# Relative-position terms of an attention block: from tables in DRAM to slices of one table on chip

## The chip, the cores and the metric

The kernel runs on one core of one Trainium2 chip. The metric is the device time of one execution, in microseconds, as the median of several runs. The core has a tensor engine (PE; its weight loads are listed apart as PEld), a vector engine (DVE), a scalar engine (ACT), GpSimd (POOL), and queues that issue DMAs; SP issues nearly all of them here, ACT's queue a few.

## The reference, cut to what matters

The whole computation has four layers on an image of 48 x 48 tokens with 768 channels: an attention block with an MLP, a spectral layer (AFNO), a state-space scan, and a second spectral layer. Only the attention block's position terms are touched. With 12 heads of 64 channels:

```python
coords = jnp.arange(H)[:, None] - jnp.arange(H)[None, :] + (H - 1)
Rh = rel_pos_h[coords]            # (48, 48, 64), from a table of 95 rows
Rw = rel_pos_w[coords]
rel_h = jnp.einsum('bhwc,hkc->bhwk', r_q, Rh)
rel_w = jnp.einsum('bhwc,wkc->bhwk', r_q, Rw)
attn = (attn.reshape(B * nh, H, W, H, W) + rel_h[:, :, :, :, None] + rel_w[:, :, :, None, :])
```

So each query gives, for each head, 48 numbers by key row and 48 by key column. All queries in one image row use the same 48 rows of the first table, a window that slides by one from row to row; the same holds for image columns and the second table.

## The kernel before, in words

**The phases.** `qkv_phase` makes q, k, v and the position terms and writes them to DRAM; attention (`attention_bounded`) reads them back in chunks; projection, MLP and the other layers follow. Everything is float32 except the position terms, which are split into three bfloat16 parts.

**The qkv phase.** Tokens are in six blocks of 384, taken two at a time as three superblocks `sb`. For each superblock `v_rows` makes v (L164, in a seven-product scheme, 21 groups of three products each), and `q_and_k` makes q and k (L295) for six pairs of heads `pr`, seven groups of three products each. The products of these two lines have weights of 128 x 128 and 384 columns.

**The position terms.** When the q of a superblock begins to be made, `position_terms` puts 24 steps on a list: first 12 `rel_h` (three pairs of pairs `cp`, two blocks `n`, two halves `hh`), then 12 `rel_w` (four image columns each). A step needs four tables of 128 x 96, one for each of four positions: two copies of the 64 x 48 window on the diagonal, one per head of the pair, zeros elsewhere. The host lays them out in DRAM (`relD`), and `tables` (L379) loads four at a time. The step makes four products (L401 for `rel_w`, L415 for `rel_h`) with 96 columns of q each into one PSUM tile of tag `m` (six buffers, shared with q, k and v). `split` then makes the three bfloat16 parts: ACT copies (L371), DVE subtracts (L372), ACT copies again (L373), DVE subtracts again (L374), into the tile `rw` or `rh`, of each of which there is one buffer. After the last step of a group, `store` (L390) writes the tile to `rw_d` or `rh_d`.

`rel_h` takes columns of q with a step of 8 floats in memory; `rel_w` takes runs of 8 floats.

**The order.** One step at a time goes between groups of q/k or v products: `advance` runs the next step, and keeps three steps' tables loading ahead. In `q_and_k` it is called twice per pair from the third pair on, eight times in all; in `v_rows` of the next superblock, `between` calls it after each group until the list is empty. Of the last superblock eight steps run among its q/k products and 16 are left. The program is written in a layer that adds the waits and allots the buffers. [...]

**The end of the phase.** After the last q/k product, DVE reduces maxima of q, k and the tables (L462 to L471); one product (L475, `bound`) sums them; DVE makes a `flag` from it (L478), by which attention chooses its form. Then four steps are issued, the phase's left-side pools are closed, five steps follow, `ahead(1)` opens attention's buffers and loads its first chunk (one piece of q, eight loads of position terms: L519, L498, L499), and the last seven steps come. An earlier `ahead(0)` has loaded the first pair's keys and values (L514, L515). Attention's first products are L559; it then adds the position terms by a product with a one-hot matrix (L567), and multiplies the values (L588).

Of the kernel before, what the change touches and what calls it, by code (L numbers as in the profile page):

```python
# [20 lines left out]
P = 128  # L21
G = 48
T = G * G
C = 768
NC = C // P
NT = T // P
NH, HD = 12, 64
FF = 4 * C
NF = FF // P
TB = 384  # L30
# [147 lines left out]
            emit(*blocks[n], o)  # L178


def qkv_phase(tc, ident, x, qkv_w, qkv_b, relT, rel_d, ln_g, ln_b, q_d, k_d, v_d, rw_d, rh_d, wqk_d, wv_d, flag, home, ahead):

# [13 lines left out]
    nc = tc.nc  # L196
    V = nc.vector
    NSB = NTB // 2
    TS = 2 * TB
    with (  # L200
# [139 lines left out]
        with tc.tile_pool(name="qkv_v0", bufs=1, side="right") as vp:  # L340
            w = vp.tile([P, 7, NC2, TB], F32, tag="wv", name="wv")
            a21 = vp.tile([P, NC2, TB], F32, tag="a21", name="a21")
            load_x(0, 0)
            for k in range(2):
                nc.sync.dma_start(w[:, k], wv[:, k * NC2 : (k + 1) * NC2, 2 * C : 2 * C + TB])
            prepare(0, 0)
            load_x(0, 1)
            nc.sync.dma_start(w[:, 6], wv[:, NC2:, 2 * C + TB :])
            nc.sync.dma_start(a21, wv[:, :NC2, 2 * C + TB :])
            vb = load_bcast(nc, kp, qkv_b[2 * C : 3 * C], C, "vb")  # L350
            qkb = load_cols(nc, kp, qkv_b[0 : 2 * C], 2 * NC, "qkb")
            kb = kp.tile([P, NC], F32, tag="kb", name="kb")
            rel = qp.tile([P, 2, 2 * G - 1], F32, tag="rel", name="rel")
            for s in range(2):
                nc.sync.dma_start(rel[s * HD : (s + 1) * HD], relT)
            qms, kms = (qp.tile([P, NC, NSB], F32, tag=n, name=n) for n in ("qms", "kms"))
            prepare(0, 1)
            combine(nc.gpsimd, (w[:, 0], w[:, 1], a21, w[:, 6]), w[:, 3], w[:, 2], w[:, 5], w[:, 4])
            sums(0)
            V.tensor_scalar(kb, qkb[:, NC : 2 * NC], HD**-0.5, None, ALU.mult)  # L360
            v_rows(0, lambda n: w[:, n])
            nc.sync.dma_start(wv_d, w)

        with tc.tile_pool(name="qkv_o", bufs=1, side="right") as op:
            R = 2 * G

            def split(ps, parts, n):

                r = op.tile([P, TB], F32, tag="rest", name=f"rest_{n}", bufs=2)
                r = r[:R].rearrange("p (a b c) -> p a b c", a=ps.shape[1], b=ps.shape[2])  # L370
                nc.scalar.copy(parts[0], ps)  # L371
                V.tensor_tensor(r, ps, parts[0], ALU.subtract)  # L372
                nc.scalar.copy(parts[1], r)  # L373
                V.tensor_tensor(parts[2], r, parts[1], ALU.subtract)  # L374

            def tables(which, g, n):

                d = qp.tile([P, 4, R], F32, tag="relD", name=f"relD_{which}_{g}_{n}", bufs=4)
                nc.sync.dma_start(d, rel_d[which, g])  # L379
                return d  # L380

            def position_terms(sb, q):


                q6 = q.rearrange("p c b (j w h) -> p c b j w h", j=KJ, w=KTW)
                tiles = {}

                def store(d, at, cols):
                    for s in range(2):
                        nc.sync.dma_start(d[s, :, :, sb, cols], at[s * G : (s + 1) * G].rearrange("k n c b t -> k n (c b t)"))  # L390

                def rel_w(g):

                    if g == 0:
                        tiles["rw"] = op.tile([P, 3, NC, 2, TB], BF16, tag="rw", name=f"rw_{sb}")
                    d, at = tiles.pop(("w", g)), tiles["rw"]
                    ps = pm.tile([P, 512], F32, tag="m", name=f"rw_{sb}_{g}")
                    pv = ps[:R, :TB].rearrange("p (c b w h) -> p c b w h", c=NC, b=2, w=4)
                    j, w0 = divmod(4 * g, KTW)
                    for i in range(4):  # L400
                        nc.tensor.matmul(pv[:, :, :, i, :], lhsT=d[:, i, :], rhs=q6[:, :, :, j, w0 + i, :], start=True, stop=True)  # L401
                    cols = slice(j * P + w0 * KTH, j * P + (w0 + 4) * KTH)
                    split(ps[:R, :TB].rearrange("p (c b t) -> p c b t", c=NC, b=2), [at[:R, n, :, :, cols] for n in range(3)], f"w{sb}_{g}")
                    if g == G // 4 - 1:
                        store(rw_d, at, slice(0, NC * TS))

                def rel_h(cp, n, hh):

                    if (n, hh) == (0, 0):
                        tiles["rh"] = op.tile([P, 3, 2, 2, TB], BF16, tag="rh", name=f"rh_{sb}_{cp}")  # L410
                    d, at = tiles.pop(("h", cp, n, hh)), tiles["rh"]
                    ps = pm.tile([P, 512], F32, tag="m", name=f"rh_{sb}_{cp}_{n}_{hh}")
                    for i in range(4):
                        rhs = q6[:, 2 * cp : 2 * cp + 2, n, :, :, 4 * hh + i].rearrange("p c j w -> p c (j w)")
                        nc.tensor.matmul(ps[:R, i * 2 * G : (i + 1) * 2 * G], lhsT=d[:, i, :], rhs=rhs, start=True, stop=True)  # L415
                    rows = at[:, :, :, n, :].rearrange("p s c (w h) -> p s c w h", h=KTH)
                    split(ps[:R, :TB].rearrange("p (h c w) -> p c w h", h=4, c=2), [rows[:R, k, :, :, 4 * hh : 4 * hh + 4] for k in range(3)], f"h{sb}_{cp}_{n}_{hh}")
                    if (n, hh) == (1, 1):
                        store(rh_d, at, slice(2 * cp * TS, (2 * cp + 2) * TS))

                def load(key, *args):
                    tiles[key] = tables(*args, "_".join(str(k) for k in (sb, *key)))

                for cp in range(NC // 2):
                    for n in range(2):
                        for hh in range(2):
                            key = "h", cp, n, hh
                            steps.append((lambda key=key: load(key, 0, 2 * (2 * sb + key[2]) + key[3]), lambda key=key: rel_h(*key[1:])))
                for g in range(G // 4):
                    steps.append((lambda g=g: load(("w", g), 1, g), lambda g=g: rel_w(g)))  # L430

            steps, ready = [], []

            def advance():
                while len(ready) < 3 and steps:
                    load, run = steps.pop(0)
                    load()
                    ready.append(run)
                if ready:
                    ready.pop(0)()  # L440

            slots = [0]

            def between():

                left = len(steps) + len(ready)
                slots[0] = slots[0] or 20
                for _ in range(-(-left // slots[0])):
                    advance()
                slots[0] = max(slots[0] - 1, 1)  # L450

            for sb in range(NSB):
# [4 lines left out]
                if sb + 1 < NSB:  # L457
                    load_x(sb + 1, 0)
                q_and_k(sb, lambda q: position_terms(sb, q), advance)

            qm, km = (qp.tile([P, NC], F32, tag=n, name=n) for n in ("qm", "km"))
            V.tensor_reduce(qm, qms, axis=AX.X, op=ALU.max)  # L462
            V.tensor_reduce(km, kms, axis=AX.X, op=ALU.max)
            rm = qp.tile([P, 2], F32, tag="rm", name="rm")
            V.tensor_reduce(rm, rel, axis=AX.X, op=ALU.max, apply_absolute_value=True)
            V.tensor_scalar(km, km, rm[:, 0:1], rm[:, 1:2], ALU.add, ALU.add)
            pz = qp.tile([P, 2, NC], F32, tag="pz", name="pz")
            V.memset(pz, 0.0)
# [7 lines left out]
            mx = qp.tile([1, 1], F32, tag="mx", name="mx")  # L476
            V.tensor_reduce(mx, ps[:1, : 2 * NC], axis=AX.X, op=ALU.max)
            V.tensor_scalar(flag, mx, SAFE, None, ALU.is_lt)  # L478
            for _ in range(4):
                advance()  # L480
            inner.close()
            for _ in range(5):
                advance()
            ahead(1)
            while steps or ready:
                advance()


# [794 lines left out]
def block_kernel(ctx: ExitStack, tc: tile.TileContext, a: dict):  # L1283
    nc = tc.nc
# [35 lines left out]
        nc.vector.memset(ones, 1.0)  # L1320
        ahead.extend((loads, kvs, qbs, ones, oneh))

    qkv_phase(tc, ident, x, a["qkv_w"], a["qkv_b"], a["relT"], a["relD"], a["ln1_g"], a["ln1_b"], q_d, k_d, v_d, rw_d, rh_d, wqk_d, wv_d, flag, home, load_ahead)

    def opened(name, shape, side):
        stack = ExitStack()
# [446 lines left out]
def laid_out(i):  # L1773
# [5 lines left out]
        d[k] = i[l0 + k]  # L1779

    d["relT"] = np.stack([i[l0 + "rel_pos_h"][::-1].T, i[l0 + "rel_pos_w"][::-1].T], 1)

    rel = np.zeros((2, G, 2, HD, 2 * G), np.float32)
    for pos in range(G):
        for s in range(2):
            rel[:, pos, s, :, s * G : (s + 1) * G] = d["relT"].transpose(1, 0, 2)[:, :, G - 1 - pos : 2 * G - 1 - pos]
    d["relD"] = rel.reshape(2, G // 4, 4, P, 2 * G).transpose(0, 1, 3, 2, 4)
# [34 lines left out]
```

## Time and profile before

| What | Value |
|---|---|
| Median of 3 runs | 3837.66 us (3835.54 to 3838.72) |
| The profiled execution's own time | 3841.45 us |
| Its span in the profile | 3839.7 us |
| Mean granted clock of PE | 0.986 of full |
| PE busy | 3727.7 us, 97% of the span |
| DVE / ACT / POOL busy | 2057.3 / 1142.8 / 656.5 us |
| Bytes moved by DMA | 460.43 MB, mean 120 GB/s |
| qkv phase | about 0 to 512 us |
| of it, the part after the last q/k product | 478.7 to 511.6 us |

A line of a group names the source line, engine, operation, tile written and tiles read, shapes (partitions x elements; for a product the weights' rows * columns first), and the number of instructions; behind the bar stand its busy time in us, the mean ns of one, and the engine's idle time before it with what ended that. A float32 product leaves two records. Records of PE overlap[...]; the distance from start to start is what a product costs in a full stream. A line of the order in time has start, length, engine, source line and count, and in brackets the idle time before it. A chain of waits is read back from the last instruction, at each step to what released it.

### The profile page before, as it was taken

The page shows a single profiled execution, that of the slowest core. Times are in us where ns is not written, and L with a number is a line of the kernel's source. Part 1 is how long each engine was busy: PE and PEld are TensorE (multiplying, and loading weights), DVE is VectorE, ACT ScalarE, POOL GpSimd, SP SyncE. Part 2 cuts the span into 40 slices and gives each one's busy share as a digit, 9 for nine tenths or more (in the row PEclk, how much of TensorE's full clock was granted, in tenths as well). Part 3 has the DMA queues.
Part 4 walks back from the last instruction along what each step waited for, and adds up shares of the span by engine and source line. Part 5 has one row for each costly group of instructions (what it writes and reads, how often), then busy time and mean ns, then how long its engine had stood idle before and what let it go on. Part 6 is the DMA issues. An engine that isn't in the chain of part 4 may idle for free.

```text
span 3839.7 us, 54414 instructions
## 1 busy us (share of the span) xinstructions
PE 3727.7 (97%) x22018; PEld 2255.4 (59%) x22018; DVE 2057.3 (54%) x3184; ACT 1142.8 (30%) x1908; POOL 656.5 (17%) x498
## 2 busy tenths in 40 slices
PE   7999979999999999999999999999999998999998
PEld 4666544444444444445555555555568876996685
DVE  6655456666666666555524332323325567995455
ACT  1323234444444444420310120012013356222341
POOL 3101001111111111015000000000013311981131
PEclk9999989999999999999999999999999999999999
DMA  7656563333232322124434534443454312112345
GB/s 254 211 193 194 178 184 119 113 107 128 84 112 75 115 74 91 42 71 139 151 104 136 173 107 121 133 137 104 125 166 105 108 36 93 40 33 73 97 114 155
DMA packets 266762, 460.43 MB, mean 120 GB/s; under 512 B 32941, under 2 KB 219301, under 8 KB 260007
## 3 DMA queue, kind: packets, MB, share of 16 engines
q1 hardware_dynamic: 256695, 435.93, 37.0%
q10 hardware_dynamic: 9808, 20.94, 1.5%
q8 instruction: 175, 2.87, 0.3%
q14 instruction: 84, 0.69, 0.1%
HBM read 318.49 MB, written 138.31 MB: 119 GB/s over the span
## 4 chain that ended last, share of the span: by engine, by line
PE 93%; DVE 2%; DMA 2%; issue 1%; ACT 1%; POOL 1%; SPq 0%; DVEq 0%; ACTq 0%; POOLq 0%
PE p L867 13%; PE p L930 12%; PE s L559 12%; PE av L588 12%; PE c L1183 6%; PE s L567 6%; PE qk L295 6%; PE c L1094 4%; PE v L164 3%; PE pj L164 2%; PE f_z L1489 2%; PE f_z L1488 2%; PE f_x L1453 2%; PE so L1263 2%; PE f_u L1503 2%; PE rh L415 1%
## 5 line engine op out<-in xcount | busy, mean ns | idle before, releaser
L577 DVE TENSOR_TENSOR acc<-acc,p 128x768 f32<-128x768 f32 x576 | 584.1, 1014 | 355.1 <-ACT p L569 317.1
L569 ACT ACTIVATE p<-s 128x768 f32<-128x768 f32 x648 | 478.6, 812 | 693.7 <-PE s L567 581.2
L930 PE MATMUL p<-w,h 128*128 128x384 f32 x1512 | 492.7, 486 | 0.0
L559 PE MATMUL s<-qt,kv 64*128 64x384 f32 x2592 | 478.5, 501 | 9.9 <-ACT p L569 7.7
L588 PE MATMUL av<-p,kv 128*64 128x384 f32 x2592 | 464.5, 493 | 0.0
L930 PEld LDWEIGHTS p<-w,h 128*128 128x128 f32 x1512 | 286.1, 190 | 196.9
L559 PEld LDWEIGHTS s<-qt,kv 64*128 64x128 f32 x2592 | 233.1, 187 | 250.6 <-ACT p L569 116.3
L588 PEld LDWEIGHTS av<-p,kv 128*64 128x64 f32 x2592 | 170.0, 136 | 225.2 <-issue 215.2
L867 PE MATMUL p<-x2nT,w 128*128 128x384 f32 x864 | 294.2, 490 | 3.4 <-issue 3.4
L295 PE MATMUL qk<-xnT,wqk 128*128 128x384 f32 x756 | 251.8, 490 | 5.3 <-DMA wqk<-wqk_d 5.3
L1183 PE MATMUL c<-H,bands 128*48 128x96 f32 x5632 | 242.2, 247 | 12.4 <-issue 12.4
L567 PE MATMUL s<-bt,oneh 120*128 120x384 bf16 x1296 | 249.1, 329 | 0.0
L1183 PEld LDWEIGHTS c<-H,bands 128*48 128x48 f32 x5632 | 234.6, 123 | 20.2 <-issue 12.7
L867 PEld LDWEIGHTS p<-x2nT,w 128*128 128x128 f32 x864 | 165.5, 192 | 119.5 <-issue 6.3
L867 PE MATMUL p<-xT,w 128*128 128x384 f32 x648 | 220.7, 486 | 0.0
L567 PEld LDWEIGHTS <-oneh 120*128 120x128 bf16 x1296 | 109.3, 98 | 174.6 <-issue 116.1
L295 PEld LDWEIGHTS qk<-xnT,wqk 128*128 128x128 f32 x756 | 144.3, 192 | 99.6 <-issue 7.9
L906 POOL TENSOR_TENSOR rr<-rr,ml_b 128x1152 f32<-128x1152 f32 x12 | 31.9, 2661 | 957.6 <-DMA rr<-xr_d 677.5
L862 ACT ACTIVATE h<-h,ml_b 128x384 f32<-128x384 f32 x144 | 88.3, 615 | 346.8 <-DVE h L882 174.3
L1191 POOL TENSOR_TENSOR t<-s,c 128x768 f32<-128x768 f32 x80 | 144.6, 1831 | 178.7 <-DVE s L1154 167.6
L867 PEld LDWEIGHTS p<-xT,w 128*128 128x128 f32 x648 | 123.1, 190 | 85.9
L597 DVE RECIPROCAL rec<-rs 128x384 f32<-128x384 f32 x36 | 92.1, 2558 | 100.6 <-PE rs L595 100.6
(323 smaller groups left out, 4800.6 us busy)
## 6 DMA issues: line engine op xcount, KB each, us to landing
w<-w1s_d SPq DMA_DIRECT2D x36, 768.0 KB
w<-w2s_d SPq DMA_DIRECT2D x36, 768.0 KB
bt<-rh_d SPq DMA_DIRECT2D x144, 162.0 KB
w<-w1s_d SPq DMA_DIRECT2D x36, 576.0 KB
w<-in_mlp_w_dram SPq DMA_DIRECT2D x27, 768.0 KB
wqk<-wqk_d SPq DMA_DIRECT2D x12, 1344.0 KB
yu<-f_ys SPq DMA_DIRECT2D x24, 672.0 KB
f_gt<-yu SPq DMA_DIRECT2D x24, 672.0 KB
```

The source lines that it names most:

```text
L164: nc.tensor.matmul(p[:, :TB], lhsT=rhs[n][:, c, t * P : (t + 1) * P], rhs=w[:, c, :], start=c == 0, stop=c == NC2 - 1)
L295: nc.tensor.matmul(p[:, :TB], lhsT=w[:, n, c, :], rhs=ops[sb][n][:, c, :], start=c == 0, stop=c == NC2 - 1)
L559: nc.tensor.matmul(ps[:, s, :QB], lhsT=keys[pr % 2][rows, kt * P : (kt + 1) * P], rhs=qbs[qc % 2][0][rows], start=True, stop=False)
L567: nc.tensor.matmul(ps[:, s, :QB], lhsT=oneh[:NBR, b % 3, :], rhs=qbs[qc % 2][1][:NBR, s, b // 3, j, :], start=False, stop=True)
L569: nc.scalar.activation(p, ps[:, :, :QB], AF.Exp)
L577: nc.vector.tensor_tensor(probs[c], probs[c], p, ALU.add)
L588: nc.tensor.matmul(avs[c][rows, :QB], lhsT=vals[pr % 2][:, kt, rows], rhs=p[:, s, :], start=kt == 0, stop=kt == NT - 1)
L867: nc.tensor.matmul(p[:, :TB], lhsT=w[n][:, c, :], rhs=rhs[n][:, c, :], start=c == 0, stop=c == NC2 - 1)
L930: nc.tensor.matmul(ps[t][:, :TB], lhsT=hs[left, f][:, t * P : (t + 1) * P], rhs=wt[:, f % KW2, :], start=f == 0, stop=f == NF2 - 1)
L1094: nc.tensor.matmul(ps[:K, i, :n], lhsT=v[:, c, tok : tok + K], rhs=w[:, cc, c0 : c0 + n], start=cc == NC - 1, stop=cc == 0)
L1183: nc.tensor.matmul(ps[r0 : r0 + G, k // 4, cols], lhsT=bands[:, n - GC, i, :] if gr else bands0[:, n, i, :], rhs=H[:, n, :, d : d + NPR], ...
L1191: GP.tensor_tensor(t, sc[:, ch], c1[:, m0 : m0 + GC].unsqueeze(2).to_broadcast([P, GC, RR, NPR]), ALU.mult)
```

## The change

The tables in DRAM go. Both tables of 95 entries (`relT`) stand on chip already, once on each half of the partitions, for the bound. They are now padded with 16 columns of zeros to 111, and a window of 64 columns is taken from them as weights, starting at the position in question; 48 of its 64 results are used. Where one product with a 128 x 96 table stood, two stand with weights of 64 x 64, one for each head of the pair: partitions 0 to 63 into PSUM partitions 0 to 63, and 64 to 127 into 64 to 127, of the same PSUM tile. The splits take all 128 partitions, and the stores take partitions 0 to 47 and 64 to 111.

At the end of the phase six steps now stand ahead of the bound's reductions and product; the pools are closed and `ahead(1)` follows at once, and ten steps come after it.

```diff
-            rel = qp.tile([P, 2, 2 * G - 1], F32, tag="rel", name="rel")
+            rel = qp.tile([P, 2, G - 1 + HD], F32, tag="rel", name="rel")
+            V.memset(rel[:, :, 2 * G - 1 :], 0.0)
             for s in range(2):
-                nc.sync.dma_start(rel[s * HD : (s + 1) * HD], relT)
+                nc.sync.dma_start(rel[s * HD : (s + 1) * HD, :, : 2 * G - 1], relT)
...
-                r = r[:R].rearrange("p (a b c) -> p a b c", a=ps.shape[1], b=ps.shape[2])
+                r = r.rearrange("p (a b c) -> p a b c", a=ps.shape[1], b=ps.shape[2])
...
-            def tables(which, g, n):
-                d = qp.tile([P, 4, R], F32, tag="relD", name=f"relD_{which}_{g}_{n}", bufs=4)
-                nc.sync.dma_start(d, rel_d[which, g])
-                return d
+            def terms(which, pos, out, rhs):
+                for s in range(2):
+                    rows = slice(s * HD, (s + 1) * HD)
+                    nc.tensor.matmul(out[rows], lhsT=rel[rows, which, G - 1 - pos : G - 1 - pos + HD], rhs=rhs[rows], start=True, stop=True)
...
-                        nc.sync.dma_start(d[s, :, :, sb, cols], at[s * G : (s + 1) * G].rearrange("k n c b t -> k n (c b t)"))
+                        nc.sync.dma_start(d[s, :, :, sb, cols], at[s * HD : s * HD + G].rearrange("k n c b t -> k n (c b t)"))
...
-                        nc.tensor.matmul(pv[:, :, :, i, :], lhsT=d[:, i, :], rhs=q6[:, :, :, j, w0 + i, :], start=True, stop=True)
+                        terms(1, 4 * g + i, pv[:, :, :, i, :], q6[:, :, :, j, w0 + i, :])
...
-                        nc.tensor.matmul(ps[:R, i * 2 * G : (i + 1) * 2 * G], lhsT=d[:, i, :], rhs=rhs, start=True, stop=True)
+                        terms(0, 4 * (2 * (2 * sb + n) + hh) + i, ps[:, i * 2 * G : (i + 1) * 2 * G], rhs)
...
             def advance():
-                while len(ready) < 3 and steps:
-                    load, run = steps.pop(0)
-                    load()
-                    ready.append(run)
-                if ready:
-                    ready.pop(0)()
+                if steps:
+                    steps.pop(0)()
...
                 q_and_k(sb, lambda q: position_terms(sb, q), advance)
+            for _ in range(6):
+                advance()
...
             V.tensor_scalar(flag, mx, SAFE, None, ALU.is_lt)
-            for _ in range(4):
-                advance()
             inner.close()
-            for _ in range(5):
-                advance()
             ahead(1)
-            while steps or ready:
+            while steps:
                 advance()
```

On the host the layout of `relD` goes; nothing else is touched.

More of the change, by code (lines that the diff above doesn't have):

```diff
@@ L178, in rows_in_seven, with qkv_phase @@
             emit(*blocks[n], o)
-def qkv_phase(tc, ident, x, qkv_w, qkv_b, relT, rel_d, ln_g, ln_b, q_d, k_d, v_d, rw_d, rh_d, wqk_d, wv_d, flag, home, ahead):
+def qkv_phase(tc, ident, x, qkv_w, qkv_b, relT, ln_g, ln_b, q_d, k_d, v_d, rw_d, rh_d, wqk_d, wv_d, flag, home, ahead):
     nc = tc.nc
@@ L364, in qkv_phase @@
         with tc.tile_pool(name="qkv_o", bufs=1, side="right") as op:
-            R = 2 * G
             def split(ps, parts, n):
                 r = op.tile([P, TB], F32, tag="rest", name=f"rest_{n}", bufs=2)
-                r = r[:R].rearrange("p (a b c) -> p a b c", a=ps.shape[1], b=ps.shape[2])
+                r = r.rearrange("p (a b c) -> p a b c", a=ps.shape[1], b=ps.shape[2])
                 nc.scalar.copy(parts[0], ps)
@@ L395, in rel_w @@
                         tiles["rw"] = op.tile([P, 3, NC, 2, TB], BF16, tag="rw", name=f"rw_{sb}")
-                    d, at = tiles.pop(("w", g)), tiles["rw"]
+                    at = tiles["rw"]
                     ps = pm.tile([P, 512], F32, tag="m", name=f"rw_{sb}_{g}")
-                    pv = ps[:R, :TB].rearrange("p (c b w h) -> p c b w h", c=NC, b=2, w=4)
+                    pv = ps[:, :TB].rearrange("p (c b w h) -> p c b w h", c=NC, b=2, w=4)
                     j, w0 = divmod(4 * g, KTW)
                     for i in range(4):
-                        nc.tensor.matmul(pv[:, :, :, i, :], lhsT=d[:, i, :], rhs=q6[:, :, :, j, w0 + i, :], start=True, stop=True)
+                        terms(1, 4 * g + i, pv[:, :, :, i, :], q6[:, :, :, j, w0 + i, :])
                     cols = slice(j * P + w0 * KTH, j * P + (w0 + 4) * KTH)
-                    split(ps[:R, :TB].rearrange("p (c b t) -> p c b t", c=NC, b=2), [at[:R, n, :, :, cols] for n in range(3)], f"w{sb}_{g}")
+                    split(ps[:, :TB].rearrange("p (c b t) -> p c b t", c=NC, b=2), [at[:, n, :, :, cols] for n in range(3)], f"w{sb}_{g}")
                     if g == G // 4 - 1:
@@ L410, in rel_h @@
                         tiles["rh"] = op.tile([P, 3, 2, 2, TB], BF16, tag="rh", name=f"rh_{sb}_{cp}")
-                    d, at = tiles.pop(("h", cp, n, hh)), tiles["rh"]
+                    at = tiles["rh"]
                     ps = pm.tile([P, 512], F32, tag="m", name=f"rh_{sb}_{cp}_{n}_{hh}")
@@ L414, in rel_h @@
                         rhs = q6[:, 2 * cp : 2 * cp + 2, n, :, :, 4 * hh + i].rearrange("p c j w -> p c (j w)")
-                        nc.tensor.matmul(ps[:R, i * 2 * G : (i + 1) * 2 * G], lhsT=d[:, i, :], rhs=rhs, start=True, stop=True)
+                        terms(0, 4 * (2 * (2 * sb + n) + hh) + i, ps[:, i * 2 * G : (i + 1) * 2 * G], rhs)
                     rows = at[:, :, :, n, :].rearrange("p s c (w h) -> p s c w h", h=KTH)
-                    split(ps[:R, :TB].rearrange("p (h c w) -> p c w h", h=4, c=2), [rows[:R, k, :, :, 4 * hh : 4 * hh + 4] for k in range(3)], f"h{sb}_{cp}_{n}_{hh}")
+                    split(ps[:, :TB].rearrange("p (h c w) -> p c w h", h=4, c=2), [rows[:, k, :, :, 4 * hh : 4 * hh + 4] for k in range(3)], f"h{sb}_{cp}_{n}_{hh}")
                     if (n, hh) == (1, 1):
                         store(rh_d, at, slice(2 * cp * TS, (2 * cp + 2) * TS))
-                def load(key, *args):
-                    tiles[key] = tables(*args, "_".join(str(k) for k in (sb, *key)))
                 for cp in range(NC // 2):
@@ L426, in position_terms @@
                         for hh in range(2):
-                            key = "h", cp, n, hh
-                            steps.append((lambda key=key: load(key, 0, 2 * (2 * sb + key[2]) + key[3]), lambda key=key: rel_h(*key[1:])))
+                            steps.append(lambda args=(cp, n, hh): rel_h(*args))
                 for g in range(G // 4):
-                    steps.append((lambda g=g: load(("w", g), 1, g), lambda g=g: rel_w(g)))
-            steps, ready = [], []
+                    steps.append(lambda g=g: rel_w(g))
+            steps = []
             def advance():
-                while len(ready) < 3 and steps:
-                    load, run = steps.pop(0)
-                    load()
-                    ready.append(run)
-                if ready:
-                    ready.pop(0)()
+                if steps:
+                    steps.pop(0)()
             slots = [0]
             def between():
-                left = len(steps) + len(ready)
+                left = len(steps)
                 slots[0] = slots[0] or 20
@@ L464, in qkv_phase @@
             rm = qp.tile([P, 2], F32, tag="rm", name="rm")
-            V.tensor_reduce(rm, rel, axis=AX.X, op=ALU.max, apply_absolute_value=True)
+            V.tensor_reduce(rm, rel[:, :, : 2 * G - 1], axis=AX.X, op=ALU.max, apply_absolute_value=True)
             V.tensor_scalar(km, km, rm[:, 0:1], rm[:, 1:2], ALU.add, ALU.add)
@@ L1321, in load_ahead @@
         ahead.extend((loads, kvs, qbs, ones, oneh))
-    qkv_phase(tc, ident, x, a["qkv_w"], a["qkv_b"], a["relT"], a["relD"], a["ln1_g"], a["ln1_b"], q_d, k_d, v_d, rw_d, rh_d, wqk_d, wv_d, flag, home, load_ahead)
+    qkv_phase(tc, ident, x, a["qkv_w"], a["qkv_b"], a["relT"], a["ln1_g"], a["ln1_b"], q_d, k_d, v_d, rw_d, rh_d, wqk_d, wv_d, flag, home, load_ahead)
     def opened(name, shape, side):
@@ L1781, in laid_out @@
     d["relT"] = np.stack([i[l0 + "rel_pos_h"][::-1].T, i[l0 + "rel_pos_w"][::-1].T], 1)
[L1783 to L1787, printed above, removed]
     for l, p in (("L1_", l1), ("L3_", l3)):
```

## The prediction

> **What bounds the kernel now.** I read the page's busy times first, then the 40 slices, then the tensor engine's groups and its order in time around the position terms.
>
> The page (busy us, share of the span, instructions; then the busy tenths of PE in 40 slices) and its groups of the position products (busy, mean ns of one, idle before):
>
> ```profile
> PE 3727.7 (97%) x22018; PEld 2255.4 (59%) x22018; DVE 2057.3 (54%) x3184; ACT 1142.8 (30%) x1908; POOL 656.5 (17%) x498
> ...
> PE   7999979999999999999999999999999998999998
> ```
>
> ```profile
> L415 PE MATMUL rh<-q,relD_h 128*96 128x96 f32 x288 | 55.8, 352 | 0.0
> L401 PE MATMUL rw<-q,relD_w 128*96 128x96 f32 x288 | 32.1, 264 | 9.6 <-DMA relD_w<-in_relD_dram 9.6
> ```
>
> PE is the bound; only slices 1, 6 and a few others show holes. The position products wait 9.6 us for their tables in all, so the tables as such cost little. Next, how long a step (four products, eight records, since each f32 product leaves two) occupies PE between its neighbours, in order of time:
>
> ```profile
> 344.22 0.84 PE L401 MATMUL rw<-q,relD_w 128*96 128x96 f32 x8
> 344.90 2.13 PE L164 MATMUL v<-wv,xnT 128*128 128x384 f32 x6
> 346.86 0.84 PE L401 MATMUL rw<-q,relD_w 128*96 128x96 f32 x8
> ...
> 418.99 1.56 PE L415 MATMUL rh<-q,relD_h 128*96 128x96 f32 x8
> 420.37 5.99 PE L295 MATMUL qk<-xnT,wqk 128*128 128x384 f32 x18
> ```
>
> From start to start, a `rel_w` step takes 0.68 us and the v group after it 1.96; a `rel_h` step takes 1.38, twice as much for as many columns. `rel_h` reads q with a step of 8 floats, `rel_w` in runs of 8. No idle time is shown: PE pays each of these steps in full. Last, the only place where PE does stand still around the change, the end of the qkv phase:
>
> ```profile
> 476.61 2.12 PE L295 MATMUL qk<-xnT,wqk 128*128 128x384 f32 x6
> 482.17 0.20 PE L475 MATMUL bound<-pz,onec 128*1 128x12 f32 x2 [3.44 <-DVE pz L471]
> 482.30 5.84 PE L415 MATMUL rh<-q,relD_h 128*96 128x96 f32 x32
> 487.96 2.22 PE L401 MATMUL rw<-q,relD_w 128*96 128x96 f32 x24
> 490.62 0.89 PE L401 MATMUL rw<-q,relD_w 128*96 128x96 f32 x8 [0.44 <-DMA relD_w<-in_relD_dram]
> 494.43 3.63 PE L401 MATMUL rw<-q,relD_w 128*96 128x96 f32 x24 [2.93 <-DMA relD_w<-in_relD_dram]
> 504.28 5.18 PE L401 MATMUL rw<-q,relD_w 128*96 128x96 f32 x40 [6.22 <-DMA relD_w<-in_relD_dram]
> 511.61 2.21 PE L559 MATMUL s<-qt,kv 64*128 64x384 f32 x12 [2.15 <-DVE rest_w L372]
> ```
>
> Sixteen of the 72 steps stand here, between the last q/k product (ends about 478.7) and attention's first (511.6): 32.9 us, of which PE idles 15.2.
>
> [...] Attention [...] changes between half rows (L559), the whole array (L567) and half columns (L588):
>
> ```profile
> 601.28 2.21 PE L559 MATMUL s<-qt,kv 64*128 64x384 f32 x12
> 603.42 1.15 PE L567 MATMUL s<-bt,oneh 120*128 120x384 bf16 x6
> 604.50 2.16 PE L588 MATMUL av<-p,kv 128*64 128x384 f32 x12
> 606.59 2.21 PE L559 MATMUL s<-qt,kv 64*128 64x384 f32 x12
> ```
>
> A 384-column f32 record in an undisturbed stream takes 0.323 us (18 qk records in 5.81 us in the chain). The twelve records of L559 would take 3.88 alone; start to start they take 2.14, so two halves run together: 6 x 0.323 = 1.94, and 0.20 is left over. L588: 2.09 - 1.94 = 0.15. L567 (half the passes): 1.08 - 0.97 = 0.11. [...] here both halves write one bank, in different partitions. No row of before does this (L559 writes two banks, L588 is split by columns).
>
> **The change, part by part.** The table loads go: 72 of 192 KB each, 14 MB of 460. Their worth on the path is the wait at the end alone. The other DMA stall of the phase, 5.28 us before the q/k products at 397.37, waits for wqk, issued at 380.04, behind v and position stores on SP; the last table load before it was issued at 369.5, and from 365 to 370 the DMA share was only 0.21, so no table backlog was left to slow it. I keep that stall.
>
> *The products.* Each step now has eight products of 64x64, two at a time on diagonal quarters of the array. No row shows a 64x64 product. Bounds: nearest is L1183 (128x48 weights, 96 columns, two column halves at once): 242.2 us over 5632 records, 43 ns each with its gaps filled, thus 82 to 86 ns a pair. If halves overlap, a `rel_w` step is 8 pairs x 0.082 = 0.66 us; if not, twice that. For `rel_h`, a pair costs one strided record, 174 ns (1.39/8), if the two strided reads overlap; 348 if they don't. I take overlap for both, since L559 reads two row halves at once.
>
> *The change of tiling, which the words of the change leave out.* Before, 128x96 products stood among 128x128 ones in one tiling; now each isolated step is entered (0.15) and left into 128-column f32 weights (0.20). `rel_w`: 0.66 + 0.15 against 0.68 is +0.13; the v group after it 1.94 + 0.20 against 1.96, +0.18; sum +0.31. `rel_h`: 1.39 + 0.15 against 1.38, +0.15, and +0.18 after it: +0.33. Isolated on a full PE stand 8 steps in the first superblock's q/k, and 16 + 8 in each of the next two: 24 `rel_w`, 32 `rel_h`. 24 x 0.31 + 32 x 0.33 = 18.0 us lost. [...] at 18 + 24 x 0.66 + 32 x 1.39 = 78 if nothing overlapped.
>
> *The splits* on ACT and DVE go from 96 to 128 partitions: free, since the same 384 columns cost 0.55 us on DVE with 96 partitions (L372) and with 128 (L313). The memset of the padding is one tiny DVE piece at a time when PE waits for weights; stores move the same bytes.
>
> *The end of the phase.* Bound's product waited 3.44 us for the reductions with four `rel_h` steps queued behind it on PE; now six steps go ahead of it. They do not bring attention 3.44 us nearer, because the next thing is late: step 9 reuses the single `rh` tile, and ACT's first copy waited 6.13 us for the store of `rh`, until 486.26. From there, DVE pays two subtractions per step; between 486.8 and 494.2 it did 14 of them, 0.535 each or 1.07 us a step. Without table waits 16 steps are 31 subtractions up to the last read of PSUM: 486.8 + 31 x 0.535 = 503.4. The bound's small DVE pieces (0.17 + 0.29 + 0.33 + 0.34 for `rm` + 0.30 after the product) may now fall among them, with PE's later steps behind the product: 0 to 1.5 us; take 0.7. Attention starts at about 504.1 instead of 511.6: 7.5 gained (6.5 to 9). PE makes a `rel_w` step in 0.7 us, below DVE's 1.07, so it isn't late. SP: the first chunk's nine loads no longer stand among tables but behind the second `rh` store (about 491), 4 us of issues; they should land near 500. If that cover fails, each us is lost.
>
> Sum: +18.0 - 7.5 = +10.5. The profiled execution spans 3839.7 (own time 3841.45), so 3850 and 3852; against the median of 3837.66, **3848 us**.
>
> **Rivals.** *Overlap fails for strided reads:* both halves take turns; 32 x 1.39 = 44.5 more, 3893. For it: [...] no trace row has two strided streams. Against: the halves lie in different partitions. *No overlap at all,* [...]: another 24 x 0.66, 3908. Against: L588's halves share a bank. *The tiling change costs nothing here:* only the end's gain is left, 3837.66 - 7.5 = 3830, faster. Its place is the border of each of the 56 steps; it decides below 7.5/56 = 0.13 us a step, against 0.31 to 0.33 worked out. For it: no 64x64 step is in the trace, and whether f32 weights of the whole array can be loaded ahead from there isn't shown. Against: three different changes in attention each pay. *The wqk stall goes too,* SP being free of waits for table buffers: 5.3 of idle and about 2 of half clock after it (0.50 granted from 395 to 400) off: about 3840.5, no change. *It doesn't do what it says:* the tables might have been hidden anyway; that is already my case but for the end.
>
> **From cases to numbers.** Likeliest 0.60 (own range 3840 to 3858); strided rival 0.12; no overlap 0.05; free tiling change 0.13; wqk stall 0.10. 0.2% (7.7 us) is what this kernel's runs can tell from no change. Of the likeliest, 0.45 is slower and 0.15 same; the two overlap rivals are 0.17 slower; free change 0.10 faster, 0.03 same; wqk 0.07 same, 0.03 faster. So slower 0.62, same 0.25, faster 0.13. The range 3826 to 3862 leaves out the two overlap rivals and a little at the bottom.
>
> **What would show it.** v groups after a step at 2.14 us and `rel_w` steps near 0.8, start to start (right); 1.96 and 0.68 would kill the tiling price. `rel_h` steps near 1.55, or near 2.9 if strided reads take turns. From the last q/k product to attention's first, about 25 us in place of 32.9, with ACT's wait for the `rh` store still in it. The wqk stall still near 5 us. A bound's product that holds PE over 2 us, or attention waiting for its first chunk, would make the end worse than worked out.

## The result, and the profile after

The changed kernel takes 3866.9 us (median of 4 runs, 3863.97 to 3867.22) against 3838.19 us before (4 runs, 3835.54 to 3841.08): ratio 1.0072, interval 1.0059 to 1.0085. It is slower by 28.7 us. The forecast was 3848 with a range of 3826 to 3862: the sign was right, the size was not.

The profiled execution took 3866.98 us, span 3864.2 (before 3841.45 and 3839.7), at a mean granted clock of 0.985 (before 0.986). The profiled execution of before lay 3.3 us above its median, so the difference to account for in the traces is smaller than 28.7: 24.5 us of span. The page's busy times, its group of q and k, and the same group before:

```profile
PE 3743.4 (97%) x22594; PEld 2240.7 (58%) x22594; DVE 2056.2 (53%) x3185; ACT 1144.2 (30%) x1908; POOL 654.0 (17%) x498
...
L295 PE MATMUL qk<-xnT,wqk 128*128 128x384 f32 x756 | 254.8, 494 | 14.1 <-DMA wqk<-wqk_d 14.1
```

```profile
L295 PE MATMUL qk<-xnT,wqk 128*128 128x384 f32 x756 | 251.8, 490 | 5.3 <-DMA wqk<-wqk_d 5.3
```

PE's busy time grew by 15.7 us, so the rest is idle time. One group shows where: ahead of the q/k products PE now stands idle 14.1 us for their weights `wqk`, where it stood 5.3. The position products by form, in the time up to 560 us:

```profile
L380 PE MATMUL rh<-q,rel 64*64 64x96 f32 x576 | 57.3, 352 | 0.0
L380 PE MATMUL rw<-q,rel 64*64 64x96 f32 x576 | 31.4, 254 | 1.8 <-DVE rest_w L372 1.6 <-DVE mx L471 0.3
```

Twice as many records, nearly the same busy time (57.3 against 55.8 us for `rel_h`, 31.4 against 32.1 for `rel_w`): two halves do run together, for strided reads as well. The 9.6 us of waits for tables are gone. The steps between their neighbours, in order of time:

```profile
349.13 0.88 PE L380 MATMUL rw<-q,rel 64*64 64x96 f32 x16
349.94 2.20 PE L164 MATMUL v<-wv,xnT 128*128 128x384 f32 x6
352.07 0.88 PE L380 MATMUL rw<-q,rel 64*64 64x96 f32 x16
...
500.16 1.59 PE L380 MATMUL rh<-q,rel 64*64 64x96 f32 x16
501.69 2.20 PE L295 MATMUL qk<-xnT,wqk 128*128 128x384 f32 x6
```

From start to start a `rel_w` step is 0.81 us (before 0.68), the group after it 2.13 (1.96), a `rel_h` step 1.53 (1.38). The end of the phase:

```profile
503.82 5.79 PE L380 MATMUL rh<-q,rel 64*64 64x96 f32 x64
509.43 1.50 PE L380 MATMUL rw<-q,rel 64*64 64x96 f32 x32
514.01 0.20 PE L469 MATMUL bound<-pz,onec 128*1 128x12 f32 x2 [3.08 <-DVE rest_h L372]
...
523.96 0.88 PE L380 MATMUL rw<-q,rel 64*64 64x96 f32 x16 [0.54 <-DVE rest_w L372]
530.64 4.01 PE L549 MATMUL s<-qt,kv 64*128 64x384 f32 x12 [5.80 <-DVE rest_w L372]
534.58 1.15 PE L557 MATMUL s<-bt,oneh 120*128 120x384 bf16 x6
537.47 3.90 PE L549 MATMUL s<-qt,kv 64*128 64x384 f32 x12 [1.74 <-ACT p L559]
```

The last q/k product ends at 503.89, attention begins at 530.64: 26.75 us instead of 32.89. But PE now idles 5.80 us ahead of attention, and the first two groups of `s` take 4.01 and 3.90 us; the mean granted clock from 530 to 535 is 0.57. Before, where it was 1.00 from 510 to 520, the first took 2.21, and the second:

```profile
516.64 2.32 PE L559 MATMUL s<-qt,kv 64*128 64x384 f32 x12 [1.74 <-ACT p L569]
```

The whole difference of span, stage by stage:

| Stage | Before | After | Difference |
|---|---|---|---|
| to the first q/k product of the last superblock | 378.38 | 392.06 | +13.68 |
| from there until the q/k products go on after the wait for `wqk` | 18.99 | 27.25 | +8.26 |
| from there to the last q/k product's end (8 steps) | 81.35 | 84.58 | +3.23 |
| end of the phase, to attention's first product | 32.89 | 26.75 | -6.14 |
| attention, to its last product | 1180.38 | 1182.55 | +2.17 |
| everything behind it | 2147.66 | 2150.99 | +3.33 |

The last row is not touched by the change; over the profiles of this study it lies between 2144.0 and 2151.7, so its 3.3 us are left unexplained. What the forecast lacked is the second row. The chain of waits there, first of the kernel before, then after:

```profile
380.04 17.19 DMA wqk<-wqk_d
397.23 0.14 issue
397.37 2.90 PE qk L295 x4
```

```profile
394.75 24.43 DMA wqk<-wqk_d
419.17 0.14 issue
419.31 6.00 PE qk L295 x9
```

The load is the same 1344 KB and was issued 14.7 us later, 1.0 us more than PE's delay at this point; it takes 24.43 us instead of 17.19. SP's queue after shows what is issued ahead of it (start, length of the issue), and the windows show the DMA engines (the last two columns are their busy share and GB/s; the one before is PE's clock):

```profile
387.48 3.09 SPq L390 DMA_DIRECT2D rw_d<-rw  x2
390.62 4.03 SPq L234 DMA_DIRECT2D v_d<-v_o  x1
394.75 3.90 SPq L245 DMA_DIRECT2D wqk<-wqk_d  x1
```

```profile
400.00:405.00 5.00, 5.00 (x17) 2.89 (x16) 2.94 (x5) 0.99 (x2) 0.00 (x0) 1.00 0.96 191
...
410.00:415.00 5.00, 0.00 (x0) 0.00 (x0) 0.00 (x0) 0.00 (x0) 0.00 (x0) 0.50 0.71 257
415.00:420.00 5.00, 0.69 (x1) 0.50 (x2) 0.00 (x0) 0.00 (x0) 0.00 (x0) 0.50 0.28 93
```

The `rw` store stands right ahead, two transfers of 1296 KB, one per head. In the trace's packet records (9216 bytes each, 144 per head) its first half takes 6.4 us and its second 14.4; before, 5.8 and 7.3. From 400 to 405 the engines are busy nearly all the time (0.96), though they move only 191 GB/s; then their mean share falls, to 0.71 from 410 and 0.28 from 415, while PE stands still. Its granted clock is 0.50 from 410 to 425. The bytes are the same; the second head's rows moved from partitions 48 to 95 to partitions 64 to 111.

### The profile page after: what moved, and what is told of

The parts are those of the page before. It is cut to its first block, busy times and chain, and to the rows that moved or that the text cites. A ratio compares the mean times of both kernels' runs of the same rounds, so it can differ in the third digit from the quotient of the medians.

```text
span 3864.2 us, 55406 instructions
## 1 busy us (share of the span) xinstructions
PE 3743.4 (97%) x22594; PEld 2240.7 (58%) x22594; DVE 2056.2 (53%) x3185; ACT 1144.2 (30%) x1908; POOL 654.0 (17%) x498
## 4 chain that ended last, share of the span: by engine, by line
PE 86%; DMA 4%; DVE 4%; POOL 3%; ACT 2%; issue 1%; SPq 1%; ACTq 0%; DVEq 0%; POOLq 0%
PE p L857 13%; PE p L920 12%; PE s L549 12%; PE av L578 11%; PE qk L295 6%; PE s L557 6%; PE c L1084 4%; PE v L164 3%; PE f_z L1478 2%; PE f_z L1479 2%; PE pj L164 2%; PE f_x L1443 2%; PE so L1253 2%; PE f_u L1493 2%; POOL t L1181 2%; PE rh L380 1%
## 5 line engine op out<-in xcount | busy, mean ns | idle before, releaser
L559 ACT ACTIVATE p<-s 128x768 f32<-128x768 f32 x648 | 478.5, 811 | 694.2 <-PE s L557 582.0
L549 PE MATMUL s<-qt,kv 64*128 64x384 f32 x2592 | 481.6, 504 | 13.5 <-ACT p L559 7.7
L295 PE MATMUL qk<-xnT,wqk 128*128 128x384 f32 x756 | 254.8, 494 | 14.1 <-DMA wqk<-wqk_d 14.1
```

What stands on the lines that cost most here:

```text
L295: nc.tensor.matmul(p[:, :TB], lhsT=w[:, n, c, :], rhs=ops[sb][n][:, c, :], start=c == 0, stop=c == NC2 - 1)
L549: nc.tensor.matmul(ps[:, s, :QB], lhsT=keys[pr % 2][rows, kt * P : (kt + 1) * P], rhs=qbs[qc % 2][0][rows], start=True, stop=False)
L559: nc.scalar.activation(p, ps[:, :, :QB], AF.Exp)
```

## The experiments

The theory of the layout (P): moving the second head's rows makes the `rw` store slow, `wqk` lands late behind it, and the price of the tiling changes stands as forecast. The rival: the new order of the queues without the table loads, or the products themselves, delay `wqk`, and the layout plays no part.

**The layout alone.** The kernel before, with tables of 112 columns instead of 96 (second head at rows 64 to 111); the tables still come from DRAM, 17% larger.

```diff
-            R = 2 * G
+            R = HD + G
...
-                        nc.sync.dma_start(d[s, :, :, sb, cols], at[s * G : (s + 1) * G].rearrange("k n c b t -> k n (c b t)"))
+                        nc.sync.dma_start(d[s, :, :, sb, cols], at[s * HD : s * HD + G].rearrange("k n c b t -> k n (c b t)"))
...
```

> The kernel before, whole-array products and tables in DRAM kept, with one edit: the second head's rows lie on partitions 64 to 111 instead of 48 to 95, as after the change. Theory P (the stores from these partitions are slow and hold up wqk): the second head's half of each rw store takes 12 to 14 us instead of 7 to 8, PE waits 12 to 14 us for wqk in the third superblock instead of 5.3, steps stay at 0.68 and 1.38 us, and the time is 7 to 11 us above before. Theory Q (the longer wait comes from another order on the DMA queue, since the table loads are gone): the wait stays near 5.3 us and the time within 3 us of before (tables 17% larger).

Measured: 3864.03 us, ratio 1.0063 (1.0049 to 1.0077): slower by 25. The waits of PE up to 560 us:

```profile
PE qk L295 <- DMA wqk<-wqk_d: 16.1, 2, 12.3
PE rw L401 <- DMA relD_w<-in_relD_dram: 10.3, 2, 9.1
```

With the old products, the old tiling and the old order, the wait for `wqk` grows from 5.3 us to 16.1 in two places (12.3 in the third superblock, the other in the second), and a table load of the end is waited for 9.1 us at once. The second halves of the three `rw` stores take 14.1, 14.0 and 11.0 us here. So the layout alone delays `wqk`, and the rival falls. The cost was larger than the 7 to 11 us expected. Of the 17.6 us of span in its profile, 8.4 stand ahead of the last superblock's first q/k product, with a wait of 3.8 for `wqk` that the expectation did not have; 7.0 at the wait that it had in view; and 3.0 in the end of the phase, where the tables are waited for. (The profiled execution is the fastest of the five, so it shows less than the 25 us between the medians.)

**Whole-array products from the table on chip.** The kernel after, with one 128x96 product per position again: the table holds the two heads in alternate columns, zeros between them on the other head's partitions, and the results stand on alternate partitions.

```diff
+                w = rel[:, which, G - 1 - pos : 2 * G - 1 - pos].rearrange("p k s -> p (k s)")
+                nc.tensor.matmul(out, lhsT=w, rhs=rhs, start=True, stop=True)
...
-                        nc.sync.dma_start(d[s, :, :, sb, cols], at[s * HD : s * HD + G].rearrange("k n c b t -> k n (c b t)"))
+                        nc.sync.dma_start(d[s, :, :, sb, cols], at[s : R : 2].rearrange("k n c b t -> k n (c b t)"))
...
```

> The kernel after with whole-array products again, but from one table on chip in which the two heads' entries alternate, so that 96 neighbouring columns are both windows; the heads' rows then lie on even and odd partitions up to 95. No change of tiling, no tables from DRAM, end of the phase as after. Theory P and the tiling price together: steps and their neighbours at 0.68 + 1.96 and 1.38 us as before, wqk wait at 5 us or less, 26 to 28 us from the last q/k product to attention; 0 to 8 us below before, 3830 to 3838. If only the tiling price counts and the wait comes from the missing tables (Q): the wait stays near 13 us, and the time is 3842 to 3850.

Measured: 3820.14 us, ratio 0.9948 (0.9934 to 0.9961): 46.8 us below the kernel after, 19 below before, and 10 below the range expected. The order of PE's work at a `rel_w` step and at the `wqk` wait, and then SP's issue of that load:

```profile
339.51 0.84 PE L383 MATMUL rw<-q,rel 128*96 128x96 f32 x8
340.19 2.13 PE L164 MATMUL v<-wv,xnT 128*128 128x384 f32 x6
342.15 0.84 PE L383 MATMUL rw<-q,rel 128*96 128x96 f32 x8
...
391.06 14.11 PE L296 MATMUL qk<-xnT,wqk 128*128 128x384 f32 x43 [1.05 <-DMA wqk<-wqk_d]
```

```profile
376.41 1.66 SPq L246 DMA_DIRECT2D wqk<-wqk_d  x1
```

The step is back at 0.68 and the group after it at 1.96, and the wait for `wqk` is 1.05. Both halves of the stores are short (second half 7.1 and 5.5 us of the first and second). Of the 46.9 us of span between the two profiles, 33.7 lie ahead of the last q/k product's end, 1.6 in the end of the phase and 7.4 in attention (1175.1 against 1182.6); the other 4.3 stand behind it, in the part that nothing here touches. In attention, a stall of 5.97 us in the first head, which before and after have alike, is gone. There, after, PE waits for ACT, ACT 10.90 us for a piece that POOL makes from a weight (5.75 here), and POOL, by the trace, for a load of position terms (`bt<-rh_d`). Behind the last `rw` store, the first loads in front of it are issued in some 2.1 us each here, and in 3.9 after; but before has the stall too, with issues of 3.0 us and less. Why it is gone stays open.

**Half as many tiling changes.** The kernel after, with two steps at every second place: 28 isolated places instead of 56.

```diff
-                if steps:
+                turn[0] += 1
+                for _ in range(min(len(steps), 2 if turn[0] % 2 == 0 else 0)):
```

> The kernel after with the same 64x64 products, but two steps at a time in every second place, so that 28 instead of 56 places change the tiling. If each change costs the 0.35 us worked out: 28 x 0.35 = 10 us below after, near 3857, with the wait for wqk unchanged. If the extra time per step lay in the 64x64 products themselves: no change, 3867.

Measured: 3853.31 us, ratio to before 1.0034 (1.0021 to 1.0048), 13.6 below the kernel after.

```profile
342.37 1.54 PE L380 MATMUL rw<-q,rel 64*64 64x96 f32 x32
343.84 4.14 PE L164 MATMUL v<-wv,xnT 128*128 128x384 f32 x12
347.91 1.54 PE L380 MATMUL rw<-q,rel 64*64 64x96 f32 x32
```

Two steps and two groups take 5.54 us here; singly they take 2 x 2.94 = 5.88. That is 0.34 us for one pair of changes. From the first v product (40.63 us after, 39.29 here) to the last superblock's first q/k product, 24 places fewer save 9.4 us, 0.39 each. The total fell by more than the 10 us expected; 1.2 us of it are a shorter wait for `wqk` (12.3). The tiling price is per place, not per product.

**The store later.** The kernel after, with the `rw` stores of the first two superblocks issued in the second step of the next superblock, behind the `wqk` loads.

```diff
-                        store(rw_d, at, slice(0, NC * TS))
+                        put = lambda: store(rw_d, at, slice(0, NC * TS))
+                        late.append(put) if sb + 1 < NSB else put()
...
+                    if (cp, n, hh) == (0, 0, 1) and late:
+                        late.pop()()
...
```

> The kernel after with one edit: the rw stores of the first two superblocks are issued some 30 us later, in the next superblock's second position step. Theory P or any in which the store stands ahead of wqk in the DMA queues: the wait for wqk at the third superblock's second pair goes from 13.5 to under 3 us, unless it comes back at a later pair; time 8 to 16 us below after, 3851 to 3859. If the load of the first pair's keys and values is what fills the queues: the wait stays above 8 us and the time within 4 us of after.

Measured: 3844.73 us, ratio 1.0012 (1.0003 to 1.002), 22 below the kernel after and below the range expected. No wait for `wqk` is left, though the first pair's values are still loaded right ahead of it, so that rival falls. PE goes through:

```profile
384.83 3.07 PE L164 MATMUL v<-wv,xnT 128*128 128x384 f32 x9
387.74 14.68 PE L295 MATMUL qk<-xnT,wqk 128*128 128x384 f32 x45
```

The last q/k product ends at 482.92 instead of 503.89: 21 us from moving two stores. Beyond the wait, PE no longer runs its next groups slowly (0.33 us a record in the 45 above; 0.67 after, 9 in 6.00 us, at a granted clock of 0.50), and short waits after the first superblock's store (2.4 us, most of them transposes waiting for their copies) are gone too. This is more than the 13.5 us that the profile files under `wqk`.

**The same for the kernel before.**

> The kernel before with the rw stores of its first two superblocks issued in the next superblock's second position step, as in the late-store run. If its own wait for wqk (5.3 us, and about 2 us of low clock after it) comes from the store ahead of it: the wait goes under 2 us, and the time is 5 to 9 us below before, 3830 to 3834. If the load of keys and values makes it: unchanged.

Measured: 3828.97 us, ratio 0.9976 (0.9966 to 0.9985): the stall of before hung on the same store, and moving the two stores was worth 9 us. PE goes through here as well:

```profile
377.99 22.42 PE L295 MATMUL qk<-xnT,wqk 128*128 128x384 f32 x69
```

With both stores out of the way, the change costs 3844.73 - 3828.97 = 15.8 us (14.7 if each is set against the runs of before that were made beside it). These two profiles also test the price of the tiling. Up to the last superblock's first q/k product they differ by 387.74 - 377.99 = 9.7 us. In that stretch the late kernel before still waits 3.5 us (transposes near 198 us, a table at 352) and has a lower granted clock near 200 (0.99 from 190 to 200, 0.84 from 200 to 210): one v group takes 3.65 us from start to start there instead of 1.96, a loss of 1.7. The late kernel after does neither, at 1.00 in both stretches. 9.7 + 3.5 + 1.7 = 14.9 us for 48 places, 0.31 each.

**The halves in the other order.** The kernel after, with the second head's half stored first.

```diff
-                    for s in range(2):
+                    for s in (1, 0):
```

> The kernel after with the two halves of each position store issued in the other order, second head first. If partitions 64 to 111 as such make the second half slow (11 to 14 us against 6), the half that is issued first is now the slow one, wqk is no nearer, and its wait stays within 2 us of 13.54 us: total about 3867. If a half is slow because it is issued second, behind another, head 0's half becomes the slow one. If the slow half only suffers from what is issued after it, both become about 9 us.

Measured: 3860.65 us (2 runs), ratio 1.0062 (1.0043 to 1.008). PE's wait, and then the chain:

```profile
PE qk L295 <- DMA wqk<-wqk_d: 8.7, 1, 8.7
```

```profile
393.48 19.86 DMA wqk<-wqk_d
```

None of the three readings holds alone. Partitions 64 to 111, stored first, take 6.0 us at the second superblock's store; partitions 0 to 47, now second, take 10.7, against 14.4 for 64 to 111 in that place (at the first superblock's: 10.9 against 14.3). So the half in the second place is the slow one, with the v store and `wqk` issued behind it, and it is slower when it is 64 to 111. Partitions as such are not slow. In the second place ahead of the v store and `wqk`, a half took 14.4 us on 64 to 111, 10.7 on 0 to 47, 7.3 on 48 to 95 (before) and 5.5 on alternate partitions (the whole-array version); at the last superblock's store, with other loads behind it, 0 to 47 and 64 to 111 take 10.8 and 11.0. What about the partitions makes these differences, no run here shows. Why 64 to 111 suffers more ahead of the v store and `wqk` stays open.

**The end with the old order.** The kernel after, with the bound ahead of the steps, as before.

> The kernel after with the end of the phase in the order of before: the bound's product first, then four steps, the pools closed, five steps, the first chunk's loads, seven steps. If the shorter end (26.8 us against 32.9) comes from the table loads being gone: 26 to 29 us again, and the time within 3 us of after. If it comes from the bound's product standing later: 30 us or more, and 3 to 6 us slower than after.

Measured: 3864.84 us, ratio 1.007 (1.0056 to 1.0084); the end takes 28.99 us. Of the 6.14 us that the end became shorter, moving the bound brought 2.2; the other 3.9 came with the rest of the change, which took away 9.59 us of waits for tables there (0.44, 2.93 and 6.22). In the total the 2.2 can't be told from nothing.

**The low clock at attention's start.** Four runs put products that nothing reads behind the last step, to fill PE's idle time. In the first two they are:

```diff
...
+            for _ in range(8):
+                nc.tensor.matmul(ps[:, :TB], lhsT=ident, rhs=qs[-1][:, 0, 0, :], start=True, stop=True)
```

> The kernel after with eight products of 384 columns added behind the last position step; their results are read by nothing. They fill about 5.2 of the 5.8 us in which PE stands still before attention. If that idle time is what lets the granted clock fall to 0.5 for attention's first two groups (4.01 and 3.90 us instead of 2.21): these groups take 2.2 us and the time is 2 to 4 us below after, 3863 to 3865. If the slow start of attention has another cause: unchanged, 3867.

> The whole-array version with the alternating table on chip, with the eight filling products of the fill run behind its last position step. Its PE stands still 6.2 us before attention. If the clock at attention's start is the cause of the slow first groups: 2 to 4 us below the version without them, 3816 to 3818; if not, unchanged at 3820.

These two missed their place: they need only q, and were put forward to the time of the `wqk` wait. Measured: 3863.1 and 3823.69 us; idle time ahead of attention still 5.70 and 6.19, so these two don't test it. The next two read a part of `rw` that a late step makes, so they stand at the end:

```diff
...
+            for _ in range(16):
+                nc.tensor.matmul(ps[:, :TB], lhsT=at[:P, 0, 0, 0, :P], rhs=at[:P, 0, :, :, 224:256], start=True, stop=True)
```

> The kernel after with 16 products of 128x384 bf16, whose result nothing reads, behind the last position step; they read a part of rw that a late step writes, so they can't be moved ahead. They should stand where PE idles for 5.80 us before attention. If that idle time is what lets attention's first two groups of s run at half clock (4.01 and 3.90 us instead of 2.21), these go to about 2.2 each, attention's own time falls by 3.5 us, and the total is some 2 to 4 us below the kernel after's 3866.9: about 3864. If the low clock has another cause, the two groups stay near 4 and the total at 3867 or above it.

> The whole-array version (x3_full96) with the same 16 unread products at the end of the position steps. By the theory of the idle time: first two groups of s from 4.21 and about 3.9 us to about 2.2 each, the total 2 to 4 us below x3_full96's 3820.1, so about 3817; otherwise 3820 or slightly above.

Measured: 3861.07 us (3856.92 to 3862.53) and 3818.86 us (3815.32 to 3821.97). From the first of these:

```profile
523.24 1.64 PE L482 MATMUL fill<-rw 128*128 128x384 bf16 x9
528.94 3.65 PE L555 MATMUL s<-qt,kv 64*128 64x384 f32 x12 [4.06 <-issue]
...
535.41 2.32 PE L555 MATMUL s<-qt,kv 64*128 64x384 f32 x12 [1.74 <-ACT p L565]
```

The filling took 1.7 us off the idle time, not all of it. The second group is fast here, but so it is after 5.70 us idle in the run with eight products, and after 6.19 in the whole-array version without any (the expectation above, about 3.9, had that wrong); in the whole-array version with 16 products, after 4.56 us idle, both groups are slow (3.90 and 3.81). The first is slow in every run with 4 us of idle or more (3.65 to 4.21), and was not with 2.15 us or less (2.21). So in these runs idle time of 4 us or more goes with a slow first group; what decides over the second isn't settled, and the lower totals can't be put down to it: of the 9.2 us of span between the profiles of the kernel after with and without the 16 products, only 1 lies in attention and 6.5 in the untouched part behind it. Neither total (5.8 and 1.3 us lower) is shown to be a gain of the filling.

## Why the prediction was wrong, by its own steps

- **PE sets the time, and the tables cost little as such:** right. The waits for tables are gone, and the end is 3.9 us shorter without the bound's move.
- **The tiling price, +18.0:** right in size, and in that it is paid per visit. Measured at the lines: `rel_w` +0.13 and +0.17 for the group after it (0.30, forecast 0.31); `rel_h` +0.15 and +0.17 (0.32, forecast 0.33): 24 x 0.30 + 32 x 0.32 = 17.4. The first row of the table of stages shows 13.68 for 48 of the 56 (forecast 15.4): of what stands against it, a wait of 1.89 us for a transposed block at 196 us is gone. Paired steps and the two late-store profiles confirm the price. What a visit pays for, no run here tells. The prediction's 0.15 and 0.20 are what it found left over at attention's L588 and L559, and that the same holds for 64x64 products was its estimate. The records of the weight loads there last 136 ns for 64 columns (L588) and 187 for 128 (L559): they differ by the same 0.05 us, but whether the weights have to do with the price isn't shown.
- **Both halves overlap, strided too:** right. Both rivals of more than 3890 fall, and so does the free tiling change. The two halves, which write different partitions of one PSUM tile, were not held up: 576 records of `rel_w` took 31.4 us, where 288 took 32.1.
- **The splits on 128 partitions, the padding:** nothing of them shows; DVE's busy time is 2056.2 against 2057.3, ACT's 1144.2 against 1142.8.
- **"Stores move the same bytes", costed at nothing:** the step that failed. The bytes are the same, but the second head moved by 16 partitions; the store's second half went from 7.3 to 14.4 us. In the kernel before with this layout alone it took 14.0.
- **"I keep that stall" (5.28 us before the q/k products):** false, as a consequence. The prediction named the queue, "behind v and position stores on SP", and asked only whether the table loads had an effect on it. The stall became 13.54 us, and with the low clock after it (0.50 from 420 to 425) 8.9 us were added: 8.26 in the second row of the stages, and 0.67 of the third, whose other 2.56 are eight `rel_h` steps at 0.32. A store costed at nothing needs its cover named: here PE's work had no slack for it, since a load that PE awaited stood behind it. With the stores moved, no stall was left.
- **The end, 32.9 to about 25 us:** 26.75; ACT's wait for the `rh` store is 1.4 us, not 6.1 as the prediction kept it; other steps' copies now stand ahead of it. The gain was 6.14, not 7.5, and 3.4 us of it were given back in attention: PE's last products end 5.80 us before attention, and two groups of `s` then take 4.01 and 3.90 us instead of 2.21 and 2.32. The prediction had low clock after the `wqk` stall (0.50) in a rival, but not here.

With the measured terms (tiling in two stretches, stall, end, attention's slow start) the sum is +13.68 + 2.56 + 8.93 - 6.14 + 3.38 = +22.41 of the 24.5 us; the rest is attention otherwise, -1.21, and the untouched part, +3.33, which lies within what single profiles differ by. The forecast had +10.5. Of the 14.0 us between, 8.9 are the stall, 3.4 the slow start of attention, 1.4 the end and 2.1 the rest; the tiling came out 1.8 cheaper.

## What to carry to other kernels

When results move to other partitions, cost their stores anew: the same bytes took 5.5 to 14.4 us here, and what counted was which load stood behind the store in its queue, and who awaited that load. Moving two stores behind the loads (22 us) or putting the heads on alternate partitions (a part of 47 us) was worth more than all that the change itself touched on PE. Small products of another tiling inside a full stream cost some 0.3 us per visit here, so gather them, or give them the neighbours' shape, even if that means multiplying zeros, as the whole-array version does.

## What the runs showed of the hardware that was not expected

- A store of 48 partitions of 27 KB each: 5.5 us on alternate partitions, 7.3 on 48 to 95, 10.7 on 0 to 47 and 14.4 on 64 to 111, all at the second superblock, in the second place ahead of the same v store and `wqk` load; in the first place 0 to 47 took 6.4 and 64 to 111 6.0.
- SP's issue of the same `wqk` load took 3.90 us after, 3.77 before, 2.38 in the late-store run and 1.66 in the whole-array version. What sets its length wasn't tried.
- A visit of four 64x64 pairs into a stream of 128x128 f32 products cost 0.30 to 0.39 us more than the products themselves.
- After 4.06 to 6.25 us without a product, the next twelve f32 records (two row halves) took 3.65 to 4.21 us; after 1.69 to 2.15 us, 2.21.
